# Cross-attention and a quantised feed-forward block on one core: down weights loaded in two steps, integers three tiles deep, a wider general path, and the parts of o behind the branch

## The chip, the cores and the metric

The kernel runs on one core of a Trainium2 chip. The metric is the device time of one execution in microseconds. Five engines work side by side, each on its own in-order queue: TensorE (PE in the profile, with PEld for its weight loads), VectorE (DVE), ScalarE (ACT), GpSimd (POOL) and SyncE (SP). SP does no arithmetic; it issues nearly all of the DMA transfers, which 16 DMA engines carry out.

## What is computed

The input `x` has 2 x 2048 rows of 512 numbers. A cross-attention over 128 context rows is added to it, and then a feed-forward block (512 to 1536 to 512) in which activations are quantised to 16 bits and weights to 4 bits in blocks of 32. Cut to what matters here:

```python
x = act_qdq(x)
up = act_qdq(x @ lpbq_dequant(w_up).T)
gate = act_qdq(x @ lpbq_dequant(w_gate).T)
sig = fixed_qdq_u16(jax.nn.sigmoid(gate))
gate = act_qdq(gate * sig)
o = act_qdq(gate * up)
return o @ lpbq_dequant(w_down).T
```

The kernel calls the last `gate` p. `act_qdq` takes the largest absolute value of the whole tensor, divides by 32767 for a scale, and rounds everything to integers of that scale. So each of these tensors has to be complete before its first integer can be made: gate before p, and up and p before o. This cuts the kernel into stages.

## The kernel before

The kernel is written in a framework that plans the order of instructions on each queue itself: the text gives a priority by its order, and an instruction whose inputs are there and whose engine is free may be placed earlier. It also sets all semaphores. Tiles come from pools; a tag with `bufs=n` has n buffers in turn.

The integers of a 16-bit tensor are split into parts of twelve bits or fewer so that float32 matmuls are exact. Each projection has two sums, `q` (parts 0 and 1) and `e` (part 2), which are joined as q times a constant minus e. Weights are split in the same way: `wd_d`, the split down weights in DRAM, holds for each of 12 chunks f a tile of 128 x 3 x 512, that is 768 KB, of which each third is one part.

The stages, in the order of time:

1. Attention and the second layer norm (`hT`), with the gate weights split beside it.
2. Gate projection, 8 groups of 512 rows by 3 sets of 4 chunks (L538 to L563). The results go to DRAM (`gate_d`), and the up and down weights are split beside it. After it, the largest gate is known.
3. Up projection (L688 to L737), 24 iterations j, each of two halves c = 2j and 2j+1 of two chunks. In iteration j: `integers_of_p(j)` (L653) makes p's integers `pi` from the gate integers `gi` and the sigmoid `sq`, and stores them to `p_d`. For each half, TensorE runs `project` (L507, L511), ACT and DVE join q and e to `u4` (L708, L709), SP stores it to `up_d` (L716), and `bound` (L661, L662) writes the row maxima of |u| times p to `pumax`. `next_gelu`, in the first half, makes `gi` and `sq` of a later tile on ACT (L593, L595, L597) and loads the gate tile after the next (L580). In the three iterations of the last group, t == 0, the down weights come in over the place of the up weights: four loads of 768 KB after each iteration (L736).
4. The scale of o. The true largest |o| isn't known without making all of o. The kernel instead takes the row and tile in which the bound is largest: `fetch_best` (L678) gathers those pieces of `up_d` and `p_d` on POOL, and from them and the last half (`u_last`) the exact products' maxima go into `two` (L752, L753). POOL reduces over partitions (L758), and a flag (L814) says whether the second-best bound shows that this is indeed the maximum.
5. If the flag says no, a general path behind a branch (L821 to L858) makes p and o anew in full. It isn't taken on these inputs, but every engine reads the flag (L820) and jumps.
6. Down projection (L860 to L891): 16 steps t of 256 rows, two tiles m each. `load_step(t)` issues six loads of p (L628), six of u (L637) and one of the residual (L639). `round_up` (L772) makes u's integers on ACT, `round_o` o's integers `oi`, `sa` and the three `parts` (L786 to L791) on DVE and ACT. TensorE runs 24 matmuls for `yq` (L877; parts 0 and 1 of the weights) and 12 for `ye` (L881; part 2), and ACT, POOL and DVE join them with the residual (L885, L887, L889) for `out` (L891).

The parts of tile m = 0 are made ahead of the branch, in three pieces:

```python
first = o_tiles(0)
round_o(first, loaded[0][0][:, :, :P], ui_first[:, :, :P], 3)

known = nc.values_load(flag[0:1, 0:1], min_val=0, max_val=1)
with tc.If(known == 0):
```

The two tile sets of `load_step` are in the pools `ld0` (opened in stage 3) and `ld1` (L764, ahead of the branch). In the general path a gate tile is one chunk of 512 columns, so 96 tiles in each of its two passes.

Of the kernel before, what the change touches and what calls it, by code (L numbers as in the profile page):

```python
# [49 lines left out]
F32 = mybir.dt.float32  # L50
# [3 lines left out]
I16 = mybir.dt.int16  # L54
# [3 lines left out]
ALU = mybir.AluOpType  # L58
# [18 lines left out]
def tile_xattn_ffn(  # L77
# [489 lines left out]
    with cp, ExitStack() as c3:  # L567
        gp2 = c3.enter_context(tc.tile_pool(name="gate", bufs=2))
        wk1 = c3.enter_context(tc.tile_pool(name="wkc1", bufs=1))
        wk2 = c3.enter_context(tc.tile_pool(name="wkc2", bufs=2))  # L570
        ps_m = c3.enter_context(tc.tile_pool(name="ps_m2", bufs=2, space=PSUM))

        def load_group(t):
# [68 lines left out]
        def next_gelu():  # L642

            j = len(ready)
            if j < len(order):
                ready.append(gelu_like(wk2, wk1, gts.pop(0), [NQ, TG], j))
                if j + 2 < len(order):
                    gts.append(load_gate(*order[j + 2]))

        def integers_of_p(j):  # L650
            gi, sq = ready[j]
            pi = wk2.tile([P, NQ, TG], I16, tag="pi", name=f"pi_{j}")
            nc.vector.scalar_tensor_tensor(pi, gi, k_p, sq, ALU.mult, ALU.mult)  # L653
# [34 lines left out]
        for j, (t, k) in enumerate(order):  # L688
            if k == 0:
                parts = groups.pop(t)  # L690
                if t + 1 < NG and t > 0:
                    groups[t - 1] = load_group(t - 1)
                if t == 0:
                    home1.__exit__(None, None, None)
                    lds.append(ctx.enter_context(tc.tile_pool(name="ld0", bufs=1, side="right")))
                    load_step(0)
            u4 = wk2.tile([P, NQ, TG], F32, tag="u4", name=f"u4_{j}")
            if j:
                pi = integers_of_p(j)
            for h in range(2):  # L700
                c = 2 * j + h
                both = slice(2 * h, 2 * h + 2)
                q = ps_m.tile([P, 2, TG], F32, tag="q", name=f"q_u{c}")
                e = ps_m.tile([P, 2, TG], F32, tag="e", name=f"e_u{c}")
                for i in range(2):
                    project(wu[NQ * k + 2 * h + i], parts, q[:, i, :], e[:, i, :])
                if c + 1 < NH:
                    nc.scalar.activation(u4[:, both, :], q, AF.Copy, scale=1.0 + 1.0 / BASE)  # L708
                    nc.vector.tensor_tensor(u4[:, both, :], u4[:, both, :], e, ALU.subtract)  # L709
                else:  # L710
                    for i in range(2):
                        v = u_last[:, i, :]
                        nc.scalar.activation(v, q[:, i, :], AF.Copy, scale=1.0 + 1.0 / BASE)
                        nc.vector.tensor_tensor(v, v, e[:, i, :], ALU.subtract)
                        abs_max(umax[:, LAST + 1 + i : LAST + 2 + i], v)
                nc.sync.dma_start(out=up_d[c], in_=u4[:, both, :] if c + 1 < NH else u_last)  # L716
                if h == 0:
                    next_gelu()
                if c == 0:
                    pi = integers_of_p(0)  # L720
                    next_gelu()
                if c + 2 < NH:
                    bound(c, u4[:, both, :], pi[:, both, :])
                elif c + 2 == NH:
                    with tc.high_priority():

                        u_last = bound(c, u4[:, both, :], pi[:, both, :])
                        ub, pb = fetch_best()
            if j < LAST:
                abs_max(umax[:, j : j + 1], u4, AX.XY)  # L730
            else:
                abs_max(umax[:, j : j + 1], u4[:, :2, :], AX.XY)
            if t == 0:
                for f in range(NQ * k, NQ * (k + 1)):
                    w = chunk_tile([P, 3, D], "wd", f)
                    nc.sync.dma_start(out=w.bitcast(F32), in_=wd_d[f])  # L736
                    wd.append(w)  # L737


        m_u = const.tile([P, 1], F32, name="m_u")  # L740
# [7 lines left out]
        two = const.tile([P, 3], F32, name="two")  # L748
        last = [v.rearrange("p i t -> p (i t)") for v in (u_last, pi[:, 2:, :])]
        for i, (uv, pv) in enumerate([last, (ub, pb)]):  # L750
            ui = wk2.tile([P, NQ, TG], I16, tag="gi", name=f"ui_b{i}").rearrange("p i t -> p (i t)")[:, : 2 * TG]
            nc.scalar.activation(ui, uv, AF.Abs, scale=r_u)  # L752
            nc.vector.tensor_tensor_reduce(uv, ui, pv, 1.0, 0.0, ALU.mult, ALU.max, two[:, i : i + 1])  # L753
            if i == 0:
                nc.vector.tensor_scalar(two[:, 2:3], best[:, 1:2], r_u, 1.0 + 2.0**-18, ALU.mult, ALU.mult)
                nc.vector.tensor_scalar(two[:, 2:3], two[:, 2:3], 0.5 * (QMAX + 2.0), None, ALU.add)
# [4 lines left out]
    with ExitStack() as c5:  # L761
        wk1 = c5.enter_context(tc.tile_pool(name="wkd1", bufs=1))
        wki = c5.enter_context(tc.tile_pool(name="wki", bufs=2))
        lds.append(c5.enter_context(tc.tile_pool(name="ld1", bufs=1)))  # L764
        wk2 = c5.enter_context(tc.tile_pool(name="wkd2", bufs=2))
        ps_y = c5.enter_context(tc.tile_pool(name="ps_y", bufs=4, space=PSUM))

        def up_tile(t):
            return wk1.tile([P, NF, TD], I16, tag="ui5", name=f"ui5_{t}")

        def round_up(ui, uv):
            nc.scalar.activation(ui, uv, AF.Copy, scale=r_u)  # L772

        def o_tiles(m):
            return (
# [30 lines left out]
            nc.vector.tensor_scalar(e_o, s_o, -BASE, None, ALU.mult)  # L806

        ui_first = up_tile(0)
        round_up(ui_first[:, :, :P], loaded[0][1][:, :, :P])
        a_o = const.tile([P, 1], F32, name="a_o")  # L810
        nc.vector.tensor_tensor(a_o, top[:, 0:1], top[:, 1:2], ALU.max)
        flag = const.tile([P, 1], I32, name="flag")
        with tc.high_priority():
            nc.vector.scalar_tensor_tensor(flag, top[:, 2:3], floor, a_o, ALU.max, ALU.is_le)  # L814
        scales_of_o(a_o)

        first = o_tiles(0)
        round_o(first, loaded[0][0][:, :, :P], ui_first[:, :, :P], 3)

        known = nc.values_load(flag[0:1, 0:1], min_val=0, max_val=1)  # L820
        with tc.If(known == 0):  # L821
            with tc.tile_pool(name="gen", bufs=1) as gp:
                pmax = gp.tile([P, NG * NF], F32, name="pmax")
                omax = gp.tile([P, NG * NF], F32, name="omax")

                def half(m, src):

                    c = (NG - 1 - m // NF) * NF + m % NF
                    return src[c // 2, :, c % 2, :]

                def load(m, src, name):
                    v = gp.tile([P, TG], F32, tag="v", name=f"v{name}_{m}")
                    nc.sync.dma_start(out=v, in_=src)
                    return v

                for m in range(NG * NF):
                    gi, sq = gelu_like(gp, gp, load(m, gate_d[m // NQ, :, m % NQ, :], "g"), [TG], f"a{m}")
                    pv = gp.tile([P, TG], F32, tag="pv", name=f"pv_{m}")
                    nc.vector.scalar_tensor_tensor(pv, gi, s_g16, sq, ALU.mult, ALU.mult)
                    abs_max(pmax[:, m : m + 1], pv)  # L840
# [4 lines left out]
                for m in range(NG * NF):  # L845
                    gi, sq = gelu_like(gp, gp, load(m, gate_d[m // NQ, :, m % NQ, :], "g"), [TG], f"b{m}")
                    pv = gp.tile([P, TG], I16, tag="pw", name=f"pw_{m}")
                    nc.vector.scalar_tensor_tensor(pv, gi, k_p, sq, ALU.mult, ALU.mult)
                    nc.sync.dma_start(out=half(m, p_d), in_=pv)
                    uw = gp.tile([P, TG], I16, tag="uw", name=f"uw_{m}")  # L850
                    nc.scalar.activation(uw, load(m, half(m, up_d), "u"), AF.Copy, scale=r_u)
                    ov = gp.tile([P, TG], F32, tag="pv", name=f"ov_{m}")
                    nc.vector.tensor_tensor(ov, pv, uw, ALU.mult)
                    abs_max(omax[:, m : m + 1], ov)
                a, = over_partitions(omax, name="om")
                load_p(0, loaded[0][0])
                scales_of_o(a)
                round_o(first, loaded[0][0][:, :, :P], ui_first[:, :, :P])  # L858

        for t in range(NT // TD):  # L860
            if t + 1 < NT // TD:
                load_step(t + 1)
            pi, uv, x1 = loaded.pop(t)
            ui = up_tile(t) if t else ui_first
            w = slice(0 if t else P, TD)
            round_up(ui[:, :, w], uv[:, :, w])
            for j in range(TD // P):
                m = t * (TD // P) + j
                if m:
                    parts = round_o(o_tiles(m), pi[:, :, ts(j, P)], ui[:, :, ts(j, P)])  # L870
                else:
                    parts = first[2]
                q = ps_y.tile([P, D], F32, tag="q", name=f"yq_{m}")
                e = ps_y.tile([P, D], F32, tag="e", name=f"ye_{m}")
                for f in range(NF):
# [39 lines left out]
```

## Time and profile before

| what | us |
|---|---|
| device time, median of 3 runs (1031.87 to 1032.9) | 1032.0 |
| device time of the profiled execution | 1033.99 |
| its span, from first to last instruction | 1032.2 |
| TensorE busy | 950.3 (92%) |
| DVE busy | 798.0 (77%) |
| ACT busy | 541.8 (52%) |
| POOL busy | 79.9 (8%) |
| mean granted TensorE clock | 0.965 |
| DMA, mean over the span | 260 GB/s |

A row of the timeline reads: start, duration, engine, line, operation, output<-inputs, shapes, count, and in brackets how long the engine was idle before and what ended that. A queue (SPq, ACTq) stands for the sequencer of an engine, which also runs waits, branches and DMA issues. In the table of DMA issues, "to landing" is the time from the issue to the last byte's semaphore. In the page's slices each digit stands for 1/40 of the span, 25.8 us.

### The profile page before, as it was taken

How to read it: one execution, taken by the hardware profiler on the slowest of the kernel's cores; microseconds unless marked ns; L12 is line 12 of the kernel's file. 1: busy time of each engine (PE TensorE's matmuls, PEld its weight loads, DVE VectorE, ACT ScalarE, POOL GpSimd, SP SyncE). 2: the span in 40 equal slices, each digit the busy share in tenths (PEclk: the TensorE clock that was granted, in tenths of full speed). 3: DMA queues.
4: the chain of work that ended last, by engine and by line, in shares of the span. 5: the costliest groups of instructions: out<-in, count | busy, mean ns of one | idle time of the engine just before them, and what ended most of it. 6: DMA issues, size and time to landing. Idle time of an engine off the chain costs nothing. (4 is left out here: it accounts for less than half of the span.)

```text
span 1032.2 us, 11748 instructions
## 1 busy us (share of the span) xinstructions
PE 950.3 (92%) x4321; PEld 764.7 (74%) x4321; DVE 798.0 (77%) x968; ACT 541.8 (52%) x610; POOL 79.9 (8%) x67
## 2 busy tenths in 40 slices
PE   6997975999999999999999999999149999999998
PEld 5765743888888888877888888888137888888886
DVE  4489866899997989546988888888459987877882
ACT  2268787332333323228998888797224434344431
POOL 0101121000000000000000000000102211122111
PEclk9999996999999999999999999999669999999999
DMA  9087644887895765896998998888948876766520
GB/s 335 28 317 272 239 173 199 320 326 283 319 372 178 301 207 173 290 395 254 351 353 318 351 350 303 335 326 306 412 143 267 273 230 195 223 201 204 173 75 31
DMA packets 125535, 268.47 MB, mean 260 GB/s; under 512 B 7264, under 2 KB 74848, under 8 KB 116768
## 3 DMA queue, kind: packets, MB, share of 16 engines
q1 hardware_dynamic: 124432, 263.75, 70.3%
q0 software_dynamic: 512, 2.88, 0.8%
q10 hardware_dynamic: 528, 1.05, 0.3%
q8 instruction: 34, 0.56, 0.2%
q14 instruction: 29, 0.24, 0.1%
HBM read 140.77 MB, written 126.88 MB: 259 GB/s over the span
## 5 line engine op out<-in xcount | busy, mean ns | idle before, releaser
L877 PE MATMUL yq<-wd,parts_o 128*128 128x512 f32 x768 | 182.2, 393 | 30.6 <-ACTq L821 28.8
L507 PE MATMUL q_g<-parts_g,wg 128*128 128x512 f32 x768 | 197.0, 397 | 5.0 <-ACT parts_g L225 5.0
L877 PEld LDWEIGHTS yq<-wd,parts_o 128*128 128x128 f32 x768 | 145.7, 190 | 62.2 <-ACTq L821 29.1
L507 PEld LDWEIGHTS q_g<-parts_g,wg 128*128 128x128 f32 x768 | 144.7, 190 | 38.5 <-ACT parts_g L225 6.1
L555 ACT ACTIVATE g<-q_g 128x512 f32<-128x512 f32 x96 | 57.3, 599 | 184.2 <-PE q_g L507 179.9
L507 PE MATMUL q_u<-parts_u,wu 128*128 128x512 f32 x576 | 144.5, 393 | 0.0
L507 PEld LDWEIGHTS q_u<-parts_u,wu 128*128 128x128 f32 x576 | 108.3, 188 | 24.5
L511 PE MATMUL e_g<-parts_g,wg 128*128 128x512 f32 x384 | 106.6, 396 | 0.0
L556 DVE CUSTOM_DVE_ANT_0 g<-g,e_g 128x512 f32<-128x512 f32 x96 | 64.7, 679 | 40.1 <-PE e_g L511 39.6
L881 PE MATMUL ye<-wd,parts_o 128*128 128x512 f32 x384 | 92.2, 389 | 0.0
L511 PEld LDWEIGHTS e_g<-parts_g,wg 128*128 128x128 f32 x384 | 72.4, 190 | 16.0
L881 PEld LDWEIGHTS ye<-wd,parts_o 128*128 128x128 f32 x384 | 72.1, 188 | 15.0
L511 PE MATMUL e_u<-parts_u,wu 128*128 128x512 f32 x288 | 78.1, 393 | 0.0
L885 ACT ACTIVATE yqs<-yq,q_o 128x512 f32<-128x512 f32 x32 | 22.0, 687 | 106.3 <-PE yq L877 106.3
L662 DVE CUSTOM_DVE_ANT_0 ua<-ua,pi 128x1024 f32<-128x1024 f32 x47 | 56.9, 1221 | 18.8 <-ACT ua L661 18.8
L788 ACT CAST parts_o<-sa_o 128x1536 fp32r<-128x1536 int16 (+1 forms) x34 | 47.4, 1398 | 45.1 <-PE ye L881 27.6
L887 POOL TENSOR_TENSOR qx<-yqs,x 128x512 f32<-128x512 f32 x32 | 52.9, 1654 | 222.1 <-ACT yqs L885 222.1
L653 DVE SCALAR_TENSOR_TENSOR pi<-gi,k_p,sq 128x2048 int16<-128x2048 int16 x24 | 56.4, 2350 | 16.3 <-ACT sq L597 16.2
L786 DVE SCALAR_TENSOR_TENSOR oi<-p,k_o,ui 128x1536 int16<-128x1536 int16 (+1 forms) x34 | 59.5, 1754 | 10.0 <-ACT ui L772 4.3
L709 DVE TENSOR_TENSOR u<-u,e_u 128x1024 f32<-128x1024 f32 x47 | 56.9, 1215 | 10.1 <-ACT u L708 10.1
L511 PEld LDWEIGHTS e_u<-parts_u,wu 128*128 128x128 f32 x288 | 54.1, 188 | 12.2
L889 DVE SCALAR_TENSOR_TENSOR y<-ye,e_o,qx 128x512 f32<-128x512 f32 x32 | 24.0, 750 | 50.4 <-PE ye L881 41.1
(176 smaller groups left out, 1412.1 us busy)
## 6 DMA issues: line engine op xcount, KB each, us to landing
gate_d<-g SPq DMA_DIRECT2D x24, 1024.0 KB, 6.5
u<-up_d SPq DMA_DIRECT2D x96, 256.0 KB, 4.7
up_d<-u SPq DMA_DIRECT2D x47, 512.0 KB, 6.1
gt<-gate_d SPq DMA_DIRECT2D x22, 1024.0 KB, 7.9
parts_d<-parts_g SPq DMA_DIRECT2D x6, 3072.0 KB, 11.3
parts_u<-parts_d SPq DMA_DIRECT2D x6, 3072.0 KB, 12.9
p_d<-pi SPq DMA_DIRECT2D x24, 512.0 KB, 9.0
p<-p_d SPq DMA_DIRECT2D x96, 128.0 KB, 2.8
```

What stands on the lines that cost most here:

```text
L507: nc.tensor.matmul(q, lhsT=w[:, s, c, :], rhs=parts[:, s, c, :], start=(c + s == 0), stop=(c + s == ND))
L511: nc.tensor.matmul(e, lhsT=w[:, 2, c, :], rhs=parts[:, 2, c, :], start=(c == 0), stop=(c == ND - 1))
L555: nc.scalar.activation(g4[:, i, :], q, AF.Copy, scale=1.0 + 1.0 / BASE)
L556: nc.vector.tensor_tensor_reduce(g4[:, i, :], g4[:, i, :], e, 1.0, LOWEST, ALU.subtract, ALU.max, gtop[:, m : m + 1])
L653: nc.vector.scalar_tensor_tensor(pi, gi, k_p, sq, ALU.mult, ALU.mult)
L662: nc.vector.tensor_tensor_reduce(ua, ua, pi, 1.0, 0.0, ALU.mult, ALU.max, pumax[:, c : c + 1])
L709: nc.vector.tensor_tensor(u4[:, both, :], u4[:, both, :], e, ALU.subtract)
L786: nc.vector.scalar_tensor_tensor(oi[:, c], pi[:, c], k_o, ui[:, c], ALU.mult, ALU.mult)
L788: nc.scalar.copy(parts[:, 0, c], a[:, c])
L877: nc.tensor.matmul(q, lhsT=parts[:, s, f, :], rhs=wd[f][:, s, :], start=(f + s == 0), stop=(f + s == NF))
L881: nc.tensor.matmul(e, lhsT=parts[:, 2, f, :], rhs=wd[f][:, 2, :], start=(f == 0), stop=(f == NF - 1))
L887: nc.gpsimd.tensor_tensor(qx, qs, x1[:, j, :], ALU.add)
```

## The change

Five edits, all from the up projection on:

- The loads of the down weights are split. After each of the last three iterations only the first two thirds of each chunk are loaded (512 KB, what `yq` reads); the last thirds of all 12 chunks (256 KB each, what `ye` reads) are loaded behind the loop.
- `gi`, `sq` and `pi` come from a pool of three buffers, and `next_gelu` is called once more in the second half of the first iteration, so that it runs one tile further ahead from there on.
- The general path works on gate tiles of 4 x 512 columns: 24 tiles in each pass for 96. Its reload of the first p tile goes through a tile of its own, from which DVE copies it.
- `round_o` of tile 0 moves behind the branch, into the loop, still in three pieces. The pool `ld1` is opened behind the branch too.
- The second half of the first `round_up` takes its scale from `r_late`, a copy of `r_u` made by a DVE operation that also reads `two[:, 1:2]`, so that it can't run before the gathered piece has been reduced.

```diff
+        wk3 = c3.enter_context(tc.tile_pool(name="wkc3", bufs=3))
...
-                ready.append(gelu_like(wk2, wk1, gts.pop(0), [NQ, TG], j))
+                ready.append(gelu_like(wk3, wk1, gts.pop(0), [NQ, TG], j))
...
-            pi = wk2.tile([P, NQ, TG], I16, tag="pi", name=f"pi_{j}")
+            pi = wk3.tile([P, NQ, TG], I16, tag="pi", name=f"pi_{j}")
...
                 if c == 0:
                     pi = integers_of_p(0)
+                if c < 2:
                     next_gelu()
...
-                    nc.sync.dma_start(out=w.bitcast(F32), in_=wd_d[f])
+                    nc.sync.dma_start(out=w[:, :2, :].bitcast(F32), in_=wd_d[f, :, :2, :])
                     wd.append(w)
+
+        for f in range(NF):
+            nc.sync.dma_start(out=wd[f][:, 2, :].bitcast(F32), in_=wd_d[f, :, 2, :])
...
-        lds.append(c5.enter_context(tc.tile_pool(name="ld1", bufs=1)))
...
-        def round_up(ui, uv):
-            nc.scalar.activation(ui, uv, AF.Copy, scale=r_u)
+        def round_up(ui, uv, r):
+            nc.scalar.activation(ui, uv, AF.Copy, scale=r)
...
-        round_up(ui_first[:, :, :P], loaded[0][1][:, :, :P])
+        round_up(ui_first[:, :, :P], loaded[0][1][:, :, :P], r_u)
+
+        r_late = const.tile([P, 1], F32, name="r_late")
+        nc.vector.scalar_tensor_tensor(r_late, two[:, 1:2], 0.0, r_u, ALU.mult, ALU.add)
...
-        first = o_tiles(0)
-        round_o(first, loaded[0][0][:, :, :P], ui_first[:, :, :P], 3)
...
+                def tile_of_gate(j, name):
+                    v = gp.tile([P, NQ, TG], F32, tag="v", name=f"vg_{name}{j}")
+                    t, k = order[j]
+                    nc.sync.dma_start(out=v, in_=gate_d[t * NK + k])
+                    return gelu_like(gp, gp, v, [NQ, TG], f"{name}{j}")
+
+                for j in range(NG * NK):
+                    gi, sq = tile_of_gate(j, "a")
+                    pv = gp.tile([P, NQ, TG], F32, tag="pv", name=f"pv_{j}")
...
-                load_p(0, loaded[0][0])
+                pv = gp.tile([P, NF, TD], I16, tag="v", name="p5_again")
+                load_p(0, pv)
+                nc.vector.tensor_copy(loaded[0][0], pv)
                 scales_of_o(a)
-                round_o(first, loaded[0][0][:, :, :P], ui_first[:, :, :P])
+
+        lds.append(c5.enter_context(tc.tile_pool(name="ld1", bufs=1)))
         for t in range(NT // TD):
...
-            w = slice(0 if t else P, TD)
-            round_up(ui[:, :, w], uv[:, :, w])
+            if t:
+                round_up(ui, uv, r_u)
+            else:
+                round_up(ui[:, :, P:], uv[:, :, P:], r_late)
...
-                if m:
-                    parts = round_o(o_tiles(m), pi[:, :, ts(j, P)], ui[:, :, ts(j, P)])
-                else:
-                    parts = first[2]
+                parts = round_o(o_tiles(m), pi[:, :, ts(j, P)], ui[:, :, ts(j, P)], 1 if m else 3)
```

More of the change, by code (lines that the diff above doesn't have):

```diff
@@ L750, in tile_xattn_ffn @@
         for i, (uv, pv) in enumerate([last, (ub, pb)]):
-            ui = wk2.tile([P, NQ, TG], I16, tag="gi", name=f"ui_b{i}").rearrange("p i t -> p (i t)")[:, : 2 * TG]
+            ui = wk3.tile([P, NQ, TG], I16, tag="gi", name=f"ui_b{i}").rearrange("p i t -> p (i t)")[:, : 2 * TG]
             nc.scalar.activation(ui, uv, AF.Abs, scale=r_u)
@@ L822, in tile_xattn_ffn @@
             with tc.tile_pool(name="gen", bufs=1) as gp:
[L823 to L838, printed above, removed]
+                pmax = gp.tile([P, NG * NK], F32, name="pmax")
+                omax = gp.tile([P, NG * NK], F32, name="omax")
+                def tile_of_gate(j, name):
[6 more added lines that the diff above has]
+                    pv = gp.tile([P, NQ, TG], F32, tag="pv", name=f"pv_{j}")
                     nc.vector.scalar_tensor_tensor(pv, gi, s_g16, sq, ALU.mult, ALU.mult)
-                    abs_max(pmax[:, m : m + 1], pv)
+                    abs_max(pmax[:, j : j + 1], pv, AX.XY)
                 a, = over_partitions(pmax, name="pm")
@@ L844, in tile_xattn_ffn @@
                 nc.vector.tensor_tensor(k_p, s_g16, r_p, ALU.mult)
-                for m in range(NG * NF):
-                    gi, sq = gelu_like(gp, gp, load(m, gate_d[m // NQ, :, m % NQ, :], "g"), [TG], f"b{m}")
-                    pv = gp.tile([P, TG], I16, tag="pw", name=f"pw_{m}")
+                for j in range(NG * NK):
+                    gi, sq = tile_of_gate(j, "b")
+                    pv = gp.tile([P, NQ, TG], I16, tag="pw", name=f"pw_{j}")
                     nc.vector.scalar_tensor_tensor(pv, gi, k_p, sq, ALU.mult, ALU.mult)
[L849 to L852, printed above, removed]
+                    uv = gp.tile([P, NQ, TG], F32, tag="v", name=f"vu_{j}")
+                    for h in range(2):
+                        both = slice(2 * h, 2 * h + 2)
+                        nc.sync.dma_start(out=p_d[2 * j + h], in_=pv[:, both, :])
+                        nc.sync.dma_start(out=uv[:, both, :], in_=up_d[2 * j + h])
+                    uw = gp.tile([P, NQ, TG], I16, tag="uw", name=f"uw_{j}")
+                    nc.scalar.activation(uw, uv, AF.Copy, scale=r_u)
+                    ov = gp.tile([P, NQ, TG], F32, tag="pv", name=f"ov_{j}")
                     nc.vector.tensor_tensor(ov, pv, uw, ALU.mult)
-                    abs_max(omax[:, m : m + 1], ov)
+                    abs_max(omax[:, j : j + 1], ov, AX.XY)
                 a, = over_partitions(omax, name="om")
-                load_p(0, loaded[0][0])
+                pv = gp.tile([P, NF, TD], I16, tag="v", name="p5_again")
+                load_p(0, pv)
+                nc.vector.tensor_copy(loaded[0][0], pv)
                 scales_of_o(a)
-                round_o(first, loaded[0][0][:, :, :P], ui_first[:, :, :P])
+        lds.append(c5.enter_context(tc.tile_pool(name="ld1", bufs=1)))
         for t in range(NT // TD):
```

## The prediction

> **What bounds the kernel now.** I read the page's slices first, then the windows around the hole they show, the timeline there, the rows of the branch, and last the chain of waits.
>
> ```profile
> PE   6997975999999999999999999999149999999998
> DMA  9087644887895765896998998888948876766520
> ```
>
> TensorE (PE) is full from slice 8 to the end but for slices 29 and 30, about 725 to 775 us. A gain has to come out of that hole, or out of the first stage, which the change leaves alone.
>
> ```profile
> 725.00:730.00 5.00, 1.75 (x8) 1.13 (x6) 4.86 (x10) 2.02 (x3) 0.00 (x0) 0.93 1.04 429
> 735.00:740.00 5.00, 0.00 (x0) 0.00 (x0) 0.00 (x0) 3.28 (x3) 0.00 (x0) 0.50 1.03 419
> 748.00:750.00 2.00, 0.00 (x0) 0.00 (x0) 0.00 (x0) 0.57 (x1) 0.00 (x0) 0.50 0.15 61
> 752.00:754.00 2.00, 0.00 (x0) 0.00 (x0) 1.50 (x9) 0.00 (x0) 0.33 (x1) 0.50 0.00 0
> ```
>
> In the windows (last three columns: clock, DMA share, GB/s) the hole has two halves: to 748 the DMA engines are full and all else waits; from 750 DMA is idle and something else waits.
>
> ```profile
> 726.94 0.32 SPq L716 DMA_DIRECT2D up_d<-u  x1
> 730.98 0.32 SPq L716 DMA_DIRECT2D up_d<-ua  x1
> 731.39 3.66 SPq L736 DMA_DIRECT2D wd<-wd_d  x4
> 740.51 2.10 POOL L678 DMA_INDIRECT best<-up_d,row  x1 [279.22 <-DMA wd<-wd_d]
> 749.43 1.15 ACT L752 ACTIVATE ui_b<-best,r_u 128x1024 int16<-128x1024 f32 x1 [11.15 <-DMA best<-up_d,row]
> 752.55 0.22 DVE L814 SCALAR_TENSOR_TENSOR flag<-top,floor,a_o 128x1 int32<-128x1 f32 x1
> 761.78 8.11 PE L877 MATMUL yq<-wd,parts_o 128*128 128x512 f32 x24 [28.83 <-ACTq L821]
> ```
> ```profile
> up_d<-u SPq DMA_DIRECT2D x1, 512.0 KB, 12.5
> ```
>
> The gather of `best` starts at 740.51. The row index it needs is ready at 729.7; what holds it is the last store that it reads, issued at 726.94, landing 12.5 us later at 739.4 because eight `wd` loads of 768 KB stand ahead of it. (The timeline names `wd`; the landing is that of `up_d`.) The flag F follows at 752.77, and TensorE starts 9.0 us after F.
>
> ```profile
> L821 POOLq COMPARE_BRANCH  x1: 53/53/53, 753.4 to 753.4; - x1
> L821 POOLq EVENT_SEMAPHORE  x1: 17/17/17, 753.8 to 753.8; - x1
> L821 SPq COMPARE_BRANCH  x1: 50/50/50, 757.2 to 757.2; - x1
> L821 ACTq COMPARE_BRANCH  x1: 50/50/50, 758.5 to 758.5; - x1
> L821 ACTq EVENT_SEMAPHORE  x1: 17/17/17, 761.7 to 761.7; - x1
> ```
>
> POOL is through the branch in 0.4 us; ACT takes 3.2 us from branch to next instruction, DVE 3.3 (758.6 to 761.9), SP 3.8 (757.2 to 761.0). ACT and DVE reach it only at 758.5, behind the first tile's parts.
>
> ```profile
> 767.43 3.25 DMA u<-up_d
> 770.92 2.86 ACT ui L772
> 773.77 0.59 ACT yqs L885
> 774.44 2.35 POOL qx L887
> 776.81 0.75 DVE y L889
> 781.48 5.55 PE yq L877 x23
> ```
>
> The chain says what is late next: behind the branch SP issues the loads of step 1, and tile m=2 starts at 781.48 on them, F+28.7. By tile m=4 (799.20, F+46.4) there are no more stalls, and the rest is TensorE alone, 8.16 us a tile.
>
> **What the skill says.** (1) "Runtime: NRT & Kernel Launch", Instruction fetch mechanics: instruction memory is refilled in blocks of 256 instructions with the next one fetched ahead, and a taken branch beyond this two-page window forces a fetch. The trace agrees: 0.4 us on POOL, with hardly anything in the branch's body, 3.2 to 3.8 on the three engines whose body is long. (2) "DMA: Bandwidth & Descriptors", Queues, rings and completion order: each engine goes round the queues packet by packet. The gather has its own queue and landed at 749.4 beside the last `wd` loads, so traffic queued behind it on SP's queue takes at most a share. (3) "TensorE: Matmul & The Clock Gate", Part 1: after an idle stretch the array runs at half clock until it has been busy a few us. Here clock 0.50, and the first 24 matmuls take 8.11 us for 5.60 later. Some 20 us of idle remain, so these 2.5 us stay.
>
> **The change, part by part.**
>
> *Down weights in two steps.* In each of the last three iterations four loads shrink from 768 to 512 KB; twelve loads of 256 KB follow behind the loop. Ahead of the store that holds the gather are eight chunks. In the trace's packets a row of 6,144 bytes takes 234 ns, of 4,096 159, of 2,048 84: 8 chunks x 128 rows / 16 engines x 75 ns = 4.8 us. (By bytes: 2.1 MB at 420 GB/s, 5.0.) Every issue up to the store comes over 5 us before its landing, so the queue never runs dry and the landing moves by all of it: 739.4 to 734.6, gather, L752 and flag with it, F' = 748.0. The second chain (store of `u_last`, in-place L753) lands with it at about 735.5 and is not late.
>
> The thirds cost 12 x 128/16 x 84 ns = 8.1 us of DMA behind 735.5 + 5.1 (the last four chunks), with 1.9 for the gather: landed by about 750.6. They are read in `ye`, 8 us after TensorE starts: hidden. SP keeps eight transfers outstanding, so its twelfth third goes out when the fourth has landed, near 745, before F': hidden by 3 us. All twelve chunks cost 12 x 8 x (159+84-234) ns = 0.9 us more of DMA.
>
> *All parts of o behind the branch.* Before, five of step 1's `u` loads (3.34 us of SP) and the parts of tile 0 stood between F and the branch. `ld1` is now opened behind the branch, so the loads go behind it too.
>
> *General path in wide tiles.* Not executed (no record of its lines), but the branch jumps over it. Counting the body: ACT 96x3+96x4 = 672 becomes 24x7 = 168; DVE some 500 becomes 134; SP 390 DMAs become 150, plus separate waits on each. ACT and DVE fall well under 256, SP perhaps 200 to 300. So I take POOL's passage for all three: flag to code behind the branch 1.0 us (752.77 to 753.8). Bounds: 1.0 and 1.0 + 3.2 to 3.8.
>
> Sum: DVE's scale operations end 0.65 us after the flag and it is through at F'+1.1. The first third of the parts took 2.4 us (`oi` 753.46, parts complete 755.87). The second half of `ui` (1.56 us on ACT) may stand ahead of the cast: F'+3.6 for TensorE, before F+9.0. SP is through at 1.5, but waits in L821 for outstanding transfers, the thirds, to 750.6 = F'+2.6; with eight catch-up steps (0.7 us) the first `p` load goes at F'+3.4. Six `p` and six `u` loads at 0.65 and the landing of the last, 3.25: `ui` at F'+14.0, before F+18.15. TensorE could start m=2 at F'+3.6+18.9 = 22.5; by the loads, with the 10.56 us between `ui` and m=2, at 24.6, before 28.7. So 4.1 is sure, and 5.4 if ACT takes `yqs` of tile 0 first, since it now waits for `u` then. I take 4.5.
>
> *`r_late`.* One 0.16 us DVE operation, under POOL's all-reduce (751.94 to 752.32). Nothing. Without that cover, 0.2.
>
> *gi, sq, pi three deep.* The same instructions in all; one gelu (ACT 2.00+2.00+1.90 = 5.9 us) moves from iteration 22 to the first one. At the end ACT and DVE finish up to 3 us sooner (L653 at 719.74 had waited on ACT), but the store is held by DMA, not by DVE: nothing. At the start ACT is full from 467 to 500 and TensorE already stalls 2.3 us there on L708. The gelu steps are interleaved with L708 in the trace, and PSUM holds two halves of 5.45 us: between 0 and 5.9 us, I take 0.5.
>
> Total: -4.8 - 4.5 + 0.5 = -8.8. On the profiled execution: span 1032.2 to 1023.4; its own time 1033.99 to 1025.2. That run is 2.0 above the median of the timed ones, so I subtract from the median: 1032.0 - 8.8 = 1023.2.
>
> **Rivals.**
>
> A. The thirds don't stay behind. The planner fills SP's idle time with later work that is ready: `p` loads of step 2 go out at 768.77, before the first `out` at 777.59. Placed between the stores, eight thirds put the 2.1 MB back: F later by 8 x 8 x 9 ns = 0.6. Against it: at 723.8 to 731 SP stood idle and yet `wd` 8 to 10, free by then, were not drawn ahead of `up_d`. At the worst +0.6 - 4.5 + 0.5: 1028.6; half drawn ahead 1026.
>
> B. The branch still pays its fetch. For: SP's body is near 256 with waits. ACT then starts the casts 3.2 later and SP loads at F'+5.7 instead of 3.4, `ui` at F'+16.3: 1.9 gained instead of 4.5, 1025.8.
>
> C. The gather ends only when the queue drains (750.6): F the same, SP not held by thirds, 1028. Against: with `wd` outstanding it took 8.9 us from issue, 5 of them before its first packet.
>
> D. Slower: the third gelu stands in ACT's in-order queue ahead of the second L708 (476.69). Its gate tile is issued at 470.27 and lands 5.2 to 13.7 us later, by 484 at the worst; with 5.9 us of gelu TensorE stalls up to 13.2 us. It decides above 9.3: then up to 1035.9. Against: in the trace the planner puts L708 between gelu steps.
>
> **How the numbers follow.** Main case 0.45 (1020.0 to 1025), A 0.22, B 0.18, C 0.05, D 0.08, else 0.02. Range 1020.0 to 1028.6: A, B and C lie in it, D and the tails outside. 0.2% is 2.1 us, about what a measurement tells from no change. Faster 0.88, within 0.03 (tails of A and C), slower 0.09 (D and a little).
>
> **What would show it.** L678 near 735.7 and the flag near 748.0 (the first step); wd thirds issued behind `up_d<-ua` (against A); ACT and DVE through L821 within 0.5 us of their branch (against B); first `yq` 3.6 us behind the flag, m=2 within 25; TensorE's last `q_u` still at 726 to 728 (against D). A flag above 751, or a hole near 475 over 5 us, proves me wrong.

## The result, and the profile after

The changed kernel takes 1026.6 us (median of 5 runs, 1025.0 to 1028.5) beside 1032.1 us before: ratio 0.9942, 95% interval 0.9924 to 0.9960, or 6.0 us of gain, give or take 1.9. The forecast was 1023.2 us. The sign, and the range of 1020.0 to 1028.6, held. Of the 8.8 us that were promised, about a third did not come.

The profiled execution after has a span of 1023.2 us and a time of its own of 1025.0, the fastest of its five. The one before was 2 us above its median. The two traces differ by 9.0 us, more than the kernels do, so positions are compared below from two marks: from the first `q_u` matmul (458.30 us before, 455.78 after; no line ahead of it was edited, and two kernels that are the same up to there, before and e4 below, reach it at 458.30 and 455.85) and from the end of the flag F.

The page after, busy tenths in 40 slices of the span:

```profile
PE   6997975999999999998999999999549999999998
DMA  9087545887895765897889988896978886666520
```

The windows after, in the same columns as before (the four counts are TensorE, its weight loads, VectorE, ScalarE, GpSimd; last the clock, the DMA share and GB/s):

```profile
725.00:730.00 5.00, 3.84 (x17) 2.84 (x16) 3.95 (x9) 2.04 (x3) 0.00 (x0) 1.00 1.02 397
735.00:740.00 5.00, 0.00 (x0) 0.00 (x0) 1.23 (x2) 1.09 (x1) 2.89 (x2) 0.50 1.02 402
748.00:750.00 2.00, 0.00 (x0) 0.00 (x0) 0.51 (x5) 0.78 (x1) 0.00 (x0) 0.50 0.87 317
752.00:754.00 2.00, 0.00 (x0) 0.00 (x0) 1.43 (x3) 0.00 (x0) 0.00 (x0) 0.50 0.04 12
```

The hole of TensorE is narrower. Its first half, DMA full, has GpSimd at work by 740 (the gather). The thirds fill the third window. In the fourth DMA and TensorE are idle and only VectorE has begun: something other than data is late.

The timeline after (start, duration, engine and line, operation, operands, in brackets the idle time before it and what ended it):

```profile
725.34 0.32 SPq L717 DMA_DIRECT2D up_d<-u  x1
730.26 0.32 SPq L717 DMA_DIRECT2D up_d<-ua  x1
730.67 2.31 SPq L738 DMA_DIRECT2D wd<-wd_d  x4
733.04 13.14 SPq L742 DMA_DIRECT2D wd<-wd_d  x12
736.49 1.92 POOL L679 DMA_INDIRECT best<-up_d,row  x1 [277.72 <-DMA wd<-wd_d]
744.51 1.15 ACT L757 ACTIVATE ui_b<-best,r_u 128x1024 int16<-128x1024 f32 x1 [8.42 <-DMA best<-up_d,row]
747.68 0.22 DVE L821 SCALAR_TENSOR_TENSOR flag<-top,floor,a_o 128x1 int32<-128x1 f32 x1
752.85 3.82 SPq L629 DMA_DIRECT2D p<-p_d  x6
754.93 7.22 PE L881 MATMUL yq<-wd,parts_o 128*128 128x512 f32 x24 [22.70 <-DMA p<-p_d]
```

The thirds (L742) stayed behind both stores, which rules rival A out. The store that holds the gather landed 10.1 us after its issue (12.5 before), the gather started at 736.49 and the flag ended at 747.90. The first `p` load follows only 4.95 us later and `yq` 7.0 us later (10.8 and 9.0 before).

The lines of the branch after (operation, count, shortest/median/longest ns, first and last start), and the DMA queues in the 5 us from 749 (packets, MB, share of 16 engines):

```profile
L824 SPq EVENT_SEMAPHORE  x8: 17/17/17, 751.6 to 752.2; - x8
L824 ACTq COMPARE_BRANCH  x1: 50/50/50, 748.5 to 748.5; - x1
L824 SPq COMPARE_BRANCH  x1: 50/50/50, 748.5 to 748.5; - x1
L824 POOLq EVENT_SEMAPHORE  x1: 17/17/17, 748.9 to 748.9; - x1
L824 ACTq EVENT_SEMAPHORE  x1: 17/17/17, 752.0 to 752.0; - x1
L824 DVEq EVENT_SEMAPHORE  x1: 21/21/21, 752.4 to 752.4; - x1
```
```profile
q1 hardware_dynamic: 157, 0.27, 14.7%
q14 instruction: 7, 0.06, 3.6%
```

All engines branch at 748.5 to 749.0. GpSimd goes on 0.45 us later, SyncE, ScalarE and VectorE 3.1, 3.6 and 3.4 us later, as before the change. Meanwhile the queue that carries instructions moves seven packets of 8 KB. Rival B is seen in the trace for ScalarE and VectorE. SyncE was held by the last thirds as well: they landed 2.0, 2.6 and 3.25 us behind the flag, and its first wait in L824 was over at 3.7.

At the start of the up projection the windows (columns as above) changed the other way. Before:

```profile
460.00:480.00 20.00, 17.69 (x76) 13.91 (x75) 6.96 (x18) 14.75 (x13) 0.37 (x1) 1.00 0.77 288
480.00:500.00 20.00, 20.00 (x88) 16.07 (x87) 19.93 (x18) 20.00 (x15) 0.00 (x0) 1.00 0.72 263
```

After:

```profile
460.00:480.00 20.00, 17.98 (x71) 14.18 (x71) 8.30 (x13) 17.43 (x14) 0.00 (x0) 0.91 0.76 290
480.00:500.00 20.00, 18.02 (x70) 13.93 (x69) 17.31 (x15) 20.00 (x16) 0.00 (x0) 0.91 0.68 233
```

ScalarE is full from 480 to 500 in both. After, TensorE makes 141 matmuls in these 40 us where it made 164 before. It stops three times (2.02, 1.92 and 0.49 us) instead of once (2.31). Behind each of the two long stops the granted clock is 0.50 for 3.4 us; behind the one stop of the kernel before it stays at 1.00. From its first `q_u` it needs 273.1 us for the up projection, 268.5 before.

The chain of waits after, up to tile m=2, and two lines of the timeline there:

```profile
764.54 3.55 DMA p<-p_d
768.09 3.54 DVE oi L790 x2
771.63 0.94 DVE sa_o L791 x2
772.57 1.68 DVE parts_o L793
774.29 5.55 PE yq L881 x23
```
```profile
765.19 2.86 ACT L776 ACTIVATE ui<-u,r_u 128x3072 int16<-128x3072 f32 x1 [1.90 <-DMA u<-up_d]
768.08 3.55 DVE L790 SCALAR_TENSOR_TENSOR oi<-p,k_o,ui 128x1536 int16<-128x1536 int16 x2 [1.49 <-DMA p<-p_d]
```

The chain names a `p` load for `oi`, but that one was issued at 764.50 and belongs to step 2. The `oi` of m=2 also reads `ui`, which ends at 768.05, and `ui` had waited for the last `u` load of step 1, which landed at 765.0. So the loads of step 1 are what m=2 waits for.

Tile m=2 (all of its matmuls but the first) now starts at 774.29 or F+26.4, where it was F+28.7; from the start of m=4 on (F+42.8, was F+46.4) TensorE no longer waits in either.

### The profile page after: what moved, and what is told of

Same layout as the page of the kernel before. It is cut to its first block, busy times and chain, and to the rows that moved or that the text cites. A ratio compares the mean times of both kernels' runs of the same rounds, so it can differ in the third digit from the quotient of the medians.

```text
span 1023.2 us, 11754 instructions
## 1 busy us (share of the span) xinstructions
PE 950.7 (93%) x4321; PEld 765.6 (75%) x4321; DVE 801.4 (78%) x969; ACT 541.5 (53%) x610; POOL 82.0 (8%) x67
## 5 line engine op out<-in xcount | busy, mean ns | idle before, releaser
L891 POOL TENSOR_TENSOR qx<-yqs,x 128x512 f32<-128x512 f32 x32 | 55.2, 1725 | 216.0 <-ACT yqs L889 202.9
```

The costliest lines, as they stand in the source:

```text
L891: nc.gpsimd.tensor_tensor(qx, qs, x1[:, j, :], ALU.add)
```

## The experiments

Each ran beside the kernel before. A ratio r against before is turned into microseconds as (r - 1) x 1033; medians of before were 1033.0 to 1033.6 in these sets. The table also gives marks from each profile: the up projection from first to last `q_u`/`e_u` matmul, F from the first `q_u`, and `yq` and the end of TensorE from F. The marks are those of one execution each. The last column is the mean time from one matmul's start to the next in the up projection where `parts` lies in the second of its two buffers, at full clock.

| kernel | median us | ratio (95%) | up projection | F | yq | end | ns |
|---|---|---|---|---|---|---|---|
| before | 1032.1 | 1 | 268.5 | 294.5 | +9.0 | +275.2 | 234.2 |
| changed | 1026.6 | 0.9942 (0.9924 to 0.9960) | 273.1 | 292.1 | +7.0 | +271.3 | 233.3 |
| e1 gelu two ahead | 1024.7 | 0.9923 (0.9901 to 0.9944) | 265.7 | 286.1 | +8.5 | +273.1 | 233.3 |
| e2 short general path | 1018.5 | 0.9867 (0.9843 to 0.9890) | 269.8 | 288.1 | +3.9 | +268.2 | 226.7 |
| e3 parts ahead of branch | 1030.3 | 0.9977 (0.9965 to 0.9989) | 274.0 | 292.9 | +8.5 | +273.7 | 234.2 |
| e4 before + gelu ahead | 1035.7 | 1.0018 (1.0006 to 1.0029) | 272.6 | 297.1 | +9.2 | +273.7 | 234.2 |
| e5 weights whole | 1031.3 | 0.9980 (0.9970 to 0.9990) | 272.9 | 296.9 | +6.8 | +271.1 | 233.3 |
| e6 changed + 128 bytes | 1023.2 | 0.9896 (0.9875 to 0.9917) | 270.8 | 290.2 | +7.2 | +272.3 | 226.7 |
| e7 e1 + 128 bytes | 1017.5 | 0.9849 (0.9821 to 0.9877) | 264.5 | 284.8 | +7.9 | +271.9 | 226.7 |
| e8 e2 + 128 bytes | 1022.6 | 0.9887 (0.9864 to 0.9909) | 273.7 | 291.3 | +3.9 | +268.1 | 233.3 |
| e9 before + 160 bytes | 1028.5 | 0.9959 (0.9943 to 0.9975) | 264.2 | 291.2 | +8.6 | +275.4 | 226.7 |
| e10 e7 + loops | 1019.7 | 0.9864 (0.9845 to 0.9884) | 264.5 | 285.0 | +4.3 | +275.7 | 226.7 |
| e11 changed + 64 bytes | 1025.3 (one run) | none | 271.1 | 289.3 | +8.9 | +273.7 | 229.0 |
| e12 before + 32 bytes | 1032.1 | 0.9983 (0.9972 to 0.9994) | 269.5 | 295.1 | +8.4 | +276.4 | 233.3 |

### e1: gelu two tiles ahead again

```diff
                 if c == 0:
                     pi = integers_of_p(0)
-                if c < 2:
                     next_gelu()
```

> The changed kernel with its gelu run two tiles ahead again, as before the change (the third buffers stay). Theory G: the gelu one tile further ahead keeps ScalarE from the evictions at the start of the up projection, so TensorE ends it 4.6 us later; the down weights take over the buffers that TensorE frees, so most of this reaches the flag. Then the stalls near 484 and 491 us are gone, the clock stays at 1.00 there, the flag lies about 289.7 us behind the first q_u matmul (292.12 in the changed kernel, 294.47 before), and the time is 1022 to 1024.2 us. Rival: the transfers set the flag whatever TensorE does in the up projection; then the flag stays at 292 us behind the first q_u and the time at 1026.6 within 0.7.

Measured: ratio 0.9923, 2.0 us under the changed kernel, with intervals that overlap; the median, 1024.65, is just above the range expected. The flag is at 286.1, 6.0 us sooner, where 2.4 were expected. The windows of e1:

```profile
460.00:480.00 20.00, 19.83 (x85) 15.60 (x84) 10.17 (x16) 19.25 (x15) 0.00 (x0) 1.00 0.72 277
480.00:500.00 20.00, 20.00 (x88) 16.39 (x88) 19.82 (x16) 20.00 (x16) 0.00 (x0) 1.00 0.80 289
```

What `q_u` waited for between 455 and 505 us (releaser, us, times), in the changed kernel and then in e1:

```profile
  ACT u L709: 9.3, 5
```
```profile
  ACT u L709: 0.8, 2
```

The wait is for ScalarE's eviction of the PSUM halves (L709), and it goes when the extra gelu does. (In e7 and e10, which also do without that gelu, one stop of 2.6 us stays, as before the change.) Between the flag and the end e1 loses 1.8 us of its 6.0: its flag is so early that the last thirds land at F+4.7, the branch takes 4.1 to 4.8 us under their traffic, and the first `p` load goes out at F+6.0.

### e4: the kernel before with only the gelu moved

```diff
                 if c == 0:
                     pi = integers_of_p(0)
+                if c < 2:
                     next_gelu()
```

with `gi`, `sq` and `pi` in a pool of three buffers.

> The kernel before with nothing but the gelu one tile further ahead and gi, sq and pi three deep. Theory G: TensorE ends the up projection 4 to 5 us later and the flag comes 2 to 4.6 us later than before: 1034 to 1036.7 us. Rival: the last stores, which leave 3.7 us earlier against the end of TensorE's up projection, pay it back; then 1032.1 us within 0.7.

Measured: 1.9 us slower (0.6 to 3.0), up projection 4.1 us longer, flag 2.6 us later. The rival (no change) is out, and 1.9 is just under the lowest time that the theory named.

### e5: the weights loaded whole

```diff
-                    nc.sync.dma_start(out=w[:, :2, :].bitcast(F32), in_=wd_d[f, :, :2, :])
+                    nc.sync.dma_start(out=w.bitcast(F32), in_=wd_d[f])
...
-        for f in range(NF):
-            nc.sync.dma_start(out=wd[f][:, 2, :].bitcast(F32), in_=wd_d[f, :, 2, :])
```

> The changed kernel with each chunk of the down weights loaded whole in the loop, as before the change, and no loads behind the loop. Theory W, the prediction's step 1: the store that the gather waits for, and the flag with it, come 4.8 us later (8 chunks x 128 / 16 x 75 ns), the flag at 296.9 us behind the first q_u matmul (292.13 in the changed kernel), and the time is 1031.4 us. Rival: the flag gains nothing that the rest of the weights doesn't cost again behind the branch, so the time stays at 1026.6 within 0.8.

Measured: median 1031.28 us, flag at 296.86 us. The theory holds to about a tenth in both. By the ratios the two steps are worth 3.9 us, by the medians 4.7.

### e3: the section of the branch as before

```diff
+        first = o_tiles(0)
+        round_o(first, loaded[0][0][:, :, :P], ui_first[:, :, :P], 3)
...
-        lds.append(c5.enter_context(tc.tile_pool(name="ld1", bufs=1)))
```

with the narrow general path, without `r_late`, and with `ld1` opened ahead of it.

> The changed kernel with the section of the branch as it was before the change: parts of tile 0 of o made ahead of the branch, narrow general path, second set of load buffers opened ahead. Theory: the section was worth 3.6 us (TensorE without stalls from 46.4 us after the flag before, 42.8 us in the changed kernel), so the time is about 1030.2 us. Rival: the section gives nothing at the end, since the loads of step 1 are what TensorE waits for in either; then 1026.6 us.

Measured: ratio 0.9977, 3.6 us above the changed kernel. Six traces of the new section that carry its full general path (changed, e1, e5, e6, e7, e11) end 272.2 us after the flag on average, five of the old one (before, e3, e4, e9, e12) 274.9: 2.7 us. The section is worth about 3 us.

### e2 and e8: an emptied general path

```diff
         with tc.If(known == 0):
-            with tc.tile_pool(name="gen", bufs=1) as gp:
...
+            nc.vector.tensor_scalar(s_o, s_o, 1.0, None, ALU.mult)
+            nc.scalar.copy(k_o, k_o)
```

> The changed kernel with the body of the general path replaced by one instruction on VectorE and one on ScalarE (the general path is left out; with this input it is jumped over anyway). Theory F: the 3.1 to 3.6 us that ScalarE, SyncE and VectorE lose at the branch are the fetch of instructions behind a body that is skipped. Then they pass in about 0.5 us as GpSimd and TensorE do, SyncE issues the first p load at about 2.2 us after the flag (4.95 in the changed kernel), the first yq follows at about 4.3 us (7.0), and the time is 1023.6 to 1024.2 us. Rival: the loss lies in the branch itself or in the semaphores that are caught up behind it; then nothing moves, 1026.6 us.

Measured: 1018.5 us, over twice the gain expected. The branch did what theory F said:

```profile
L824 ACTq COMPARE_BRANCH  x1: 45/45/45, 742.3 to 742.3; - x1
L824 ACTq EVENT_SEMAPHORE  x1: 17/17/17, 742.6 to 742.6; - x1
L824 DVEq COMPARE_BRANCH  x1: 72/72/72, 742.8 to 742.8; - x1
L824 DVEq EVENT_SEMAPHORE  x1: 21/21/21, 743.1 to 743.1; - x1
```

ScalarE, VectorE and SyncE go on in 0.2 to 0.4 us. SyncE gains more than the jump: the eight waits that it has in L824 in the changed kernel are not in this kernel, and its first `p` load goes out at F+1.15, for 2.2 expected, though the last third lands only at F+4.95. One instruction packet moves near the branch instead of seven, `yq` starts at F+3.9, and the end comes 3.1 us sooner after the flag. But the flag too came 4.1 us sooner, in code that was not edited. The matmuls of the up projection that read `parts` from its second buffer (every other group of 512 tokens) took 226.7 ns from start to start where they take 233.3 in the changed kernel. Those that read its first buffer took 226.7 to 227.0 ns in every run. The emptied body has fewer constants, which moves everything behind them in SBUF: the weights of the projections begin at byte 19168 of a partition in place of 19296 (19264 before the change). The second buffer stays at 204768 in all kernels; the first moves with the weights, 73,728 bytes (288 x 256) behind them. In e2 alone of these the distance from weights to second buffer is a multiple of 256 bytes. Hence e8, which takes the weights back to 19296:

```diff
-        r_late = const.tile([P, 1], F32, name="r_late")
+        r_late = const.tile([P, 33], F32, name="r_late")[:, 0:1]
```

> The run with the short general path (which is left out) once more, with 128 bytes more in the region of constants, which puts the weights at byte 19296 as in the changed kernel. Theories F and P: the branch is passed 3.1 us sooner and the matmuls of the second buffer are at 233 ns again, so the time is 1023.5 us. If the whole gain of the short general path is the branch or the shorter program, it stays at 1018.5 us.

Measured: 1022.6 us, the matmuls at 233.3 ns again and the branch still quick. Against the changed kernel the emptied body is worth 5.7 us by the ratios, with an error of 3, and 3.2 after the flag by the traces; this holds both the quicker jump and SyncE's missing waits. The rest of e2's gain, put down to where its tiles lay, is 2.1 us by the ratios, less than its error of 3.4; the flags of the two traces are 3.3 us apart.

### e6, e7, e9, e11, e12: bytes between the constants and the weights

e6 and e7 use the edit of e8, in the changed kernel and in e1, which puts the weights at 19424 (a multiple of 256 from the second buffer). e11 takes 64 bytes instead. In the kernel before, e9 adds 160 bytes and e12 32, the latter being what `r_late` adds in the change:

```diff
-        a_o = const.tile([P, 1], F32, name="a_o")
+        a_o = const.tile([P, 41], F32, name="a_o")[:, 0:1]
```

> The changed kernel with 128 bytes more in the region of constants, so that the chunks of weights begin at byte 19424 of a partition in place of 19296 and nothing else changes. Theory P: a matmul of the gate and up projections takes 233 ns from start to start where parts lies in the second of its two buffers and 226.7 ns in the first, because the weights' address and that of the second buffer (204768, which never moves) differ by something other than a multiple of 256 bytes; in the run with the short general path they happened to agree. Then all of them take 226.7 ns, 2 x 576 x 6.5 ns = 7.5 us go, and the time is 1019.1 us. Rival: the 226.7 ns of that run came from the shorter program, not from the addresses; then the time is 1026.6 us.

> The changed kernel with gelu two tiles ahead again and the same 128 bytes more. If theories G and P both hold and add, 1024.65 - 7.5 = 1017.2 us, with no stall at the start of the up projection and 226.7 ns for all matmuls; with G alone 1024.6 us, with P alone 1019.1 us.

> The kernel before with nothing but 160 bytes more in the region of constants, so that the weights begin at byte 19424 of a partition in place of 19264. Theory P: all matmuls of the gate and up projections come to 226.7 ns from 234.2 in the second buffer; 2 x 576 x 7.5 ns = 8.6 us go, less what a stall at the start of the up projection takes back (the pad in the changed kernel brought about 5 of 7.5 us): 1025 to 1028.5 us. Rival: no change, 1033 us.

> The changed kernel with 64 bytes more in the region of constants: the weights begin at byte 19360, 192 bytes behind a multiple of 256 as seen from the second buffer of parts. Theory P with a period of 256 bytes: its matmuls stay slow, 230 to 235 ns. If the period is 64 bytes, they come to 226.7 ns.

> The kernel before with 32 bytes more in the region of constants, which puts the weights at byte 19296, where the one new constant of the change (r_late) puts them. Theory P: its matmuls of the second buffer go from 234.2 to 233.2 ns, and 1152 x 1.0 ns = 1.1 us of what the change gains is this: 1031.9 us against 1033. Rival: the two differ for another reason, 234.2 ns stay, and so does the time.

One line each of a stretch in a slow group, before and in e9 (ns of one matmul, shortest/median/longest; a record is longer than the time to the next start, as matmuls overlap):

```profile
L507 PE MATMUL q_u<-parts_u,wu x80: 392/397/400, 530.2 to 557.2; 128*128 128x512 f32 x80
```
```profile
L507 PE MATMUL q_u<-parts_u,wu x78: 389/389/390, 530.4 to 556.0; 128*128 128x512 f32 x78
```

The granted clock is 1.00 in both. Modulo 256 the weights stand 96, 128, 192 and 0 bytes past the second buffer in before, the changed kernel, e11 and e6; a matmul takes 234.2, 233.3, 229.0 and 226.7 ns. (e11 was expected at 230 to 235.) e12 moved from 96 to 128, and from 234.2 to 233.3. So the dependence on placement is shown, and a period of 64 is out. That the distance between these two tiles is the cause, and not that of another pair which moves with them, is only argued.

The times follow less well than the nanoseconds. e6 is 4.8 us under the changed kernel, not 7.5. In its trace the stops at the start of the up projection grew (3.2 and 2.3 us, for 2.0 and 1.9), so that it still takes 270.8 us, and the end comes 1.0 us later behind the flag; that faster matmuls run into ScalarE's limit there is the likely reason. e9 gains 4.2 us (2.6 to 5.9) where 8.6 were worked out and 5 to 8.5 expected. e7 met its 1017.2 with 1017.5 us, though a stop of 2.6 us stayed at the start of the up projection where none was expected. It has everything the changed kernel has but the gelu a tile further ahead, and has the lowest median of all: 15.6 us under before, 9.6 under the changed kernel.

### e10: a general path of two loops

```diff
-                for j in range(NG * NK):
-                    gi, sq = tile_of_gate(j, "a")
+                with tc.For_i(0, NG, 1) as g:
+                    for k in range(NK):
+                        gi, sq = tile_of_gate(g, k, "a")
```

and likewise the second loop, on top of e7.

> The kernel with gelu two tiles ahead and the weights at byte 19424, with the general path written as two loops over the 8 groups of tokens, so that its body has 79 instructions on ScalarE, 148 on SyncE and 79 on VectorE in place of 242, 225 and 210. Theory F: a body of this length is jumped over at about the price of the emptied one (ScalarE, SyncE and VectorE at most 1 us), and the time is 1017.5 - 3.1 = 1014.4 us. Rival: SyncE's 148 instructions still need a fetch, and its loads with them: then ScalarE and VectorE pass quickly, SyncE does not, and the time is 1016 to 1017.5 us.

Measured: 1019.7 us, above both ranges; by the ratios 1.5 us slower than e7, within the error. ScalarE and VectorE pass quickly and SyncE doesn't, as the rival said:

```profile
L823 SPq EVENT_SEMAPHORE  x8: 17/17/17, 744.4 to 746.4; - x8
L823 ACTq COMPARE_BRANCH  x1: 45/45/45, 741.6 to 741.6; - x1
L823 SPq COMPARE_BRANCH  x1: 50/50/50, 741.6 to 741.6; - x1
L823 ACTq EVENT_SEMAPHORE  x1: 17/17/17, 742.0 to 742.0; - x1
```

ScalarE, with 79 instructions to jump, needs 0.46 us, VectorE 0.58 (its body has 93 in the compiled program, not the 79 expected); SyncE, with 148, goes on after 2.8. But that it needs a fetch is not shown. Its first, second and third waits are over at F+3.40, 4.06 and 5.00, and the last three thirds land at F+3.38, 4.04 and 4.98: it waits for the down weights, as the flag comes so early here. Whatever its jump took, it was hidden under that. TensorE starts at F+4.3, but the loads of step 1 go out at F+6.4, and it then stops for 4.56 us at F+23. Nothing is won over e7: the loads were the limit, and SyncE was held by the thirds.

## Why the prediction was right, and where it fell short

**Down weights in two steps (-4.8): right.** e5 isolates it: the flag moves by 4.7 us, 296.86 to 292.13. In the changed kernel's own trace this is hidden. From the first `q_u` its flag is only 2.4 us sooner, since the stall below pushed the other way; that it still stood near the 748.0 foretold came from a start 2.5 us earlier, which is luck: executions of the same code differ by as much there. The thirds were hidden from TensorE, as foretold: the last landed at 751.15, before `ye` at 761.99. For SyncE they are not free, as the next point shows.

**All parts behind the branch (-4.5): right in sign, a third too large.** It is worth 2.7 us by the traces and 3.6 by the times. The failed term is "flag to code behind the branch 1.0 us", and with it "So I take POOL's passage for all three". The wide general path cut the body, in the compiled program, from 960, 684 and 786 instructions on ScalarE, SyncE and VectorE to 242, 225 and 210 (where the estimate had 168, 200 to 300 and 134), but the passage stayed at 3.1 to 3.6 us. For TensorE's start this is the whole miss: `yq` at F+7.0 where 3.6 was foretold, and at 3.9 and 4.3 where the bodies of ScalarE and VectorE are short (e2, e10). For the loads it is a part. The last third landed at F+3.25 in place of 2.6, and would have held SyncE until then anyway; the jump made it 3.7. The first load went out at F+4.95, for 3.4 in the main case and 5.7 in rival B. From there to `ui` took 12.3 us for 10.6, since the last `u` load landed 5.0 us after its issue and not 3.25, and from `ui` to m=2 9.1 for 10.56. So rival B had the mechanism, and its place for m=2 (28.7 less 1.9 is 26.8, measured 26.4, main case 24.6) came out in part by luck: `ui` was at F+17.3, not at its 16.3. That more than this 2.3 us is left once TensorE no longer waits (42.8 for 46.4) neither case had. The step rested on the Trainium skill, "Runtime: NRT & Kernel Launch", Instruction fetch mechanics: a fetch when the target lies outside a window of two pages of 256 instructions. The runs agree that a long body costs time and a short one next to none, and packets on the instruction queue go with it. But they put the limit lower: bodies of 79 and 93 instructions were jumped in 0.5 and 0.6 us, of 210 and more in 2.6 us or more, and the packets are 8 KB. The measurement decides.

**Three buffers and a gelu further ahead (+0.5): the term that was most mis-sized.** The bounds were 0 and 5.9 us, one whole gelu on ScalarE. The traces give the upper end: with weights 96 or 128 bytes off, five runs with the gelu further ahead (changed, e3, e4, e5, e8) have an up projection of 273.3 us on average and three without (before, e1, e12) 267.9; with aligned weights it is 270.3 (e2, e6) against 264.4 (e7, e9, e10). That is 5.4 and 5.9. ScalarE is the limit in that stretch, so a gelu moved into it costs TensorE nearly its own length. What reaches the time depends on what lies behind: 1.9 us in e4, where the queue of whole weights may take part of it up; 2.0 from e1 to the changed kernel, within the error of either; 4.9 from e7 to e6. The reason given, that the planner interleaves gelu steps with the evictions, held only in part. In the changed kernel four gelu steps and a step of `bound` stand between two evictions (L709), which are 9.3 us apart; before, the two at this point were 2.8 apart (L708 at 476.69 and 479.49):

```profile
473.75 1.00 ACT L709 ACTIVATE u<-q_u 128x1024 f32<-128x1024 f32 x1
474.65 1.99 ACT L596 ACTIVATE sig<-gi,s_g 128x2048 f32<-128x2048 int16 x1
476.55 2.00 ACT L594 ACTIVATE gi<-gt,r_g 128x2048 int16<-128x2048 f32 x1
478.44 1.90 ACT L598 ACTIVATE sq<-sig 128x2048 uint16<-128x2048 f32 x1
480.24 1.05 ACT L662 ACTIVATE ua<-u 128x1024 f32<-128x1024 f32 x1
481.19 1.99 ACT L596 ACTIVATE sig<-gi,s_g 128x2048 f32<-128x2048 int16 x1
483.08 1.00 ACT L709 ACTIVATE u<-q_u 128x1024 f32<-128x1024 f32 x1
```

It was rival D in place and kind (ahead of the third eviction, not the second), at under half its price.

**`r_late` (0): wrong for a reason not thought of.** Its instruction costs nothing seen. Its tile moves the weights by 32 bytes. For the matmuls on the second buffer that is 0.9 ns less in the up projection and 0.9 to 2.0 less in the gate projection, 576 each: about 1.4 us of gain worked out from the two traces, 1.8 (0.6 to 2.9) in e12.

The terms as measured are -3.9 (e5), -3.6 (e3, which holds what `r_late` gives too) and +1.9 (e4), together -5.6; 6.0 of gain, give or take 1.9, was found. Without the 1.4 of `r_late` the section of the branch is worth 2.2, near the 2.7 of the traces. The sum is not exact, as each single gain carries 1 to 2 us of error and the stall's price depends on the rest.

## What to carry to other kernels

Where an in-order engine is full, as ScalarE was here, expect work moved forward into that stretch to cost its length, and look for a place where the engine has air. For code behind a branch, count what each engine must jump and which transfers it must still wait for, the engine that issues the next loads first. When a chain of waits names a load, see by its issue time whether it is the one that the instruction needs. And before a small gain is put down to an edit, see whether unedited matmuls changed their duration: a constant added can move every tile behind it.

## What was not expected of the hardware

- Matmuls 128x128 by 128x512 in fp32r took 226.7, 229.0, 233.3 or 234.2 ns from start to start at a granted clock of 1.00, by where the operands lay in SBUF. 160 bytes of padding alone brought the kernel before 4.2 us (2.6 to 5.9), against 6.0 for the whole change. Why is open.
- A jump took 0.2 to 0.6 us over bodies of up to 93 instructions and 2.6 to 5.3 over 210 and more; between the two nothing was measured, as SyncE's 148 in e10 are covered by its waits. Over the same body it went with late transfers: 2.8 to 3.3 us in e5 (no thirds), 3.1 to 3.6 in the changed kernel (thirds until F+3.25), 4.1 to 4.8 in e1 (until F+4.7). That sharing the DMA engines is the cause is not shown.
- A stop of TensorE of 2 us can cost more than itself, and doesn't always. In the changed kernel the granted clock was 0.50 for 3.4 us behind both long stops: the 24 matmuls behind the second took 7.44 us for 5.60 otherwise, on top of the gap of 1.92. Behind single stops of 2.3 to 2.6 us in before, e7, e9 and e10 it stayed at 1.00, in e12 it fell. What decides is open.
